# Who sums the two halves of the expert output: GpSimd, or VectorE and TensorE

## The chip, the cores and the metric

The kernel runs on one core of a Trainium2 chip, as one launch. The metric is the device time of that launch in microseconds (us), the median of several executions.

## What is computed

Two layers, each a graph attention over 2708 nodes with 256 features followed by a mixture of experts of which every row uses two. The change lies behind the last experts, in the last lines of layer 1:

```python
    def _L1_ffn_ref(x, gate_w, gate_b, w1, b1, w2, b2, gamma, beta):
        ...
        topk_vals, topk_idx = jax.lax.top_k(gate_logits, K)
        topk_w = jax.nn.softmax(topk_vals, axis=-1)
        h = jax.nn.relu(jnp.einsum('bsh,ehf->bsef', x, w1) + b1)
        expert_out = jnp.einsum('bsef,efh->bseh', h, w2) + b2
        sel = jnp.take_along_axis(expert_out, topk_idx[:, :, :, None], axis=2)
        moe = jnp.sum(topk_w[..., None] * sel, axis=2)
        y = x + moe
        mu = jnp.mean(y, axis=-1, keepdims=True)
        var = jnp.var(y, axis=-1, keepdims=True)
        return (y - mu) / jnp.sqrt(var + EPS) * gamma + beta
    ...
    x = x + _L1_ffn_ref((_layernorm(x, axis=-1))[None], ...)[0]
```

## The kernel before

The 2708 rows lie in 22 tiles: 20 of 128 rows, and tiles 20 and 21 of 74 rows each. The rows of layer 1 are sorted by expert into pages of 128, called blocks; 45 blocks (0 to 44) are computed in the main stream, and further ones only if the data needs them.

**A block.** TensorE makes the hidden activations (`hide`, L880) and the output (`sum_hidden`, L895 and L898). VectorE multiplies the output by the row's weight on its way out of PSUM (`scaled`, L902 and L904). GpSimd issues an indirect DMA that adds the 128 result rows to an array in DRAM (`add`, L909). There are two such arrays, `sums1[0]` for even blocks and `sums1[1]` for odd ones; an add into one of them waits until the previous add into the same one has landed (`last_add`). `sums1[0]` also holds the input rows, stored there before. So y of a row is `sums1[0] + sums1[1]`, and the layer norm over y is what is left to do.

**The three groups of tiles.** `EARLY_LAST` names two groups that finish while blocks still run: tiles 0 to 5 behind block 35, and tiles 6 to 11 behind block 38. `early_last` waits for the add, and for tiles 6 to 11 also until the last weights and the last rows of the blocks were asked for (`loaded`, `fetched`). It loads both halves of y into `y_all`, a view of the old mask's memory (the profile calls it `mask_t`), with L1420: `y_all[:, 0]` and `y_all[:, 1]`. GpSimd adds the halves, two tiles at a time (L1953). VectorE then takes mean and variance (`stats`: L427 and L428), 13 small operations for the inverse deviation, and two operations for each tile (L1963, L1965). The other ten tiles, 12 to 21, are `late_last`: four groups of 2, 2, 4 and 2 tiles. `load_y` asks for them behind the last block and behind the conditional. `last1` then lets GpSimd add the halves by pairs (L1990), VectorE take the statistics, ScalarE the first inverse root (`root`, L434 and L435), VectorE one Newton step (`mend`, three operations at L380), and VectorE two operations for each tile:

```python
                nc.vector.scalar_tensor_tensor(y, y_all[:r, 0, t], ln_y.mv[:r, t, 0:1],
                                               last["gamma"][:r], op0=OP.subtract, op1=OP.mult)
                nc.vector.scalar_tensor_tensor(y, y, ln_y.rstd[:r, t:t + 1], x1[:r, t, :],
                                               op0=OP.mult, op1=OP.add)
```

These are L2003 and L2005. Each pair then leaves by a store from SP's queue (L2008). The stores of tiles 6 to 11 (`early_out`, L1974) are issued on SP behind the loads of `load_y`.

**The conditional.** `experts1.rest` (L940 to L943) holds the blocks past 44 under a `tc.If`. Each engine loads the number of rows in use, compares and, as a rule, jumps over the body. An engine that jumps raises its semaphores by what the body would have raised them; that is what a row of L943 in the trace shows. GpSimd raises those of its DMA queue there too (`INC_SWDGE_SEM`). Whoever waits behind the conditional for work that could have been in the body waits for that row.

**What sets the order.** Instructions of one engine run in the order in which they are issued. That order is made by a planner in the kernel's own text, `Clock`: pieces of work are generators which yield an engine and a cost (`yield "POOL", 1.3`), a `Mark` that something is done, or a slot of a buffer (`Slots`), and the planner issues what would be ready first. `clock.moved` says when a transfer should land. The planned times shape the order only; what an instruction really waits for are semaphores. `psum_stage` opens a new set of PSUM tiles and closes the old one, so that a new tile's first use waits for the old tiles' last uses.

## Time and profile before

| what | value |
|---|---|
| time, median of 3 runs | 1156.15 us (1155.14 to 1159.67) |
| the profiled execution's own time | 1157.12 us |
| its span | 1155.4 us |
| mean granted TensorE clock | 0.949 |
| TensorE matmul busy | 1030.2 us, 89% of the span |
| VectorE busy | 542.2 us, 47% |
| ScalarE busy | 573.1 us, 50% |
| GpSimd busy | 366.2 us, 32% |

The span is that of the instructions on the core; the execution's own time holds 1.7 us more around it. TensorE's share is that of the whole kernel. The last 43 us are a stage of another kind: TensorE's last matmul of the profiled execution starts at 1112.1 us. All times of the prediction are counted from the start of the span.

### The profile page before, as it was taken

To read this page: it belongs to the slowest core of one execution; us is meant where nothing else is said; L and a number is where in the kernel's file an instruction comes from. 1 tells how busy PE (TensorE), PEld (TensorE's weight loads), DVE (VectorE), ACT (ScalarE), POOL (GpSimd) and SP (SyncE) were. 2 spreads that over 40 slices of the span, in tenths; PEclk is the share of its full clock that TensorE was granted. 3 is DMA by queue.
4 is the path that set the end of the run, shared out by engine and by line. 5 is a ranking of instruction groups with operands and counts; after the bars stand their busy time and mean duration, and the time that the engine had idled before them with its cause. 6 is when DMAs were issued, how large, how long until landed. Compare 5 with 4: busy or idle time off the path is not lost. (4 is left out here: it accounts for less than half of the span.)

```text
span 1155.4 us, 21226 instructions
## 1 busy us (share of the span) xinstructions
PE 1030.2 (89%) x6665; PEld 914.1 (79%) x6665; DVE 542.2 (47%) x2083; ACT 573.1 (50%) x1599; POOL 366.2 (32%) x417
## 2 busy tenths in 40 slices
PE   5999999997999999999999998998984888899850
PEld 3888888875789999999998954998984777798840
DVE  7678888865531111101111336647776641122368
ACT  4876667653534444444443458446753543344420
POOL 7521121111142221112223351252434355333441
PEclk9999999998999999999999999998996899899985
DMA  9965445410898999999899959401125477787973
GB/s 281 288 236 174 156 159 182 135 77 28 295 283 263 322 322 327 324 304 321 250 318 332 335 155 256 153 1 38 60 65 186 122 180 187 171 214 176 282 196 120
DMA packets 165053, 238.96 MB, mean 207 GB/s; under 512 B 10627, under 2 KB 139966, under 8 KB 162224
## 3 DMA queue, kind: packets, MB, share of 16 engines
q1 hardware_dynamic: 146116, 214.09, 56.6%
q0 software_dynamic: 18816, 23.42, 10.6%
q8 instruction: 56, 0.92, 0.3%
q14 instruction: 65, 0.53, 0.1%
HBM read 205.54 MB, written 54.99 MB: 225 GB/s over the span
## 5 line engine op out<-in xcount | busy, mean ns | idle before, releaser
L904 DVE TENSOR_SCALAR yo<-out_ps,w 128x256 f32<-128x256 f32 x92 | 44.5, 484 | 409.4 <-PE out_ps L898 408.8
L1238 PE MATMUL att_ps<-g_all,z 128*128 128x257 f32 (+3 forms) x968 | 227.3, 388 | 0.0
L1238 PEld LDWEIGHTS att_ps<-g_all,z 128*128 128x128 f32 (+3 forms) x968 | 177.3, 188 | 36.3 <-issue 8.9
L898 PE MATMUL out_ps<-room,ht 128*128 128x256 f32 x872 | 200.0, 381 | 0.0
L880 PEld LDWEIGHTS hid_ps<-xt,room 128*128 128x128 f32 x1504 | 176.2, 193 | 6.3 <-issue 3.4
L880 PE MATMUL hid_ps<-xt,room 128*128 128x128 f32 x1504 | 177.5, 277 | 3.2 <-DMA room<-in_L_ffn_W_dram 2.7
L898 PEld LDWEIGHTS out_ps<-room,ht 128*128 128x128 f32 x872 | 161.9, 191 | 21.0
L1224 ACT ACTIVATE zr<-e_bc,minus_one,g_all 128x256 f32<-128x256 f32 (+3 forms) x242 | 130.5, 591 | 59.0 <-DVE z L1227 58.3
L884 ACT ACTIVATE ht<-hid_ps,w_t 128x128 f32<-128x128 f32 x376 | 128.8, 364 | 26.7 <-PE hid_ps L880 7.4
L909 POOL DMA_INDIRECT sums<-yo,xg x43 | 66.8, 1555 | 233.7 <-DVE side L872 204.7
L674 POOL DMA_INDIRECT rows_d<-xr,place x88 | 92.3, 1049 | 123.7 <-DVE xr L443 77.0
L1638 PE MATMUL att_ps<-half,wide_mask 128*128 128x258 f32 (+1 forms) x968 | 124.5, 290 | 2.5 <-ACT h_all L1575 1.5
L1638 PEld LDWEIGHTS att_ps<-half,wide_mask 128*128 128x128 f32 (+1 forms) x968 | 121.5, 195 | 3.9 <-ACT h_all L1575 2.4
L909 POOL DMA_INDIRECT sums<-yo,xr x45 | 70.7, 1572 | 128.9 <-DVE w L902 42.7
L1227 DVE SCALAR_TENSOR_TENSOR z<-zr,mask_t 128x256 f32<-128x256 f32 (+3 forms) x242 | 96.2, 419 | 30.6 <-ACT zr L1224 17.5
L884 ACT ACTIVATE ht<-hid_ps,w1x 128x128 f32<-128x128 f32 x180 | 62.3, 363 | 95.7 <-PE hid_ps L880 92.5
L874 ACT ACTIVATE w<-xg,side 128x1 f32<-128x1 f32 x43 | 12.7, 294 | 167.5 <-DVE side L872 167.5
L1515 POOL CAST wide_mask<-mask_t 128x1408 fp32r<-128x1408 fp8e4 x31 | 42.5, 1376 | 101.6 <-PE att_ps L1638 67.5
L880 PE MATMUL hid_ps<-lo,wide_mask 128*128 128x128 f32 x480 | 65.7, 294 | 9.9 <-DMA wide_mask<-in_L_ffn_w_dram 9.0
L880 PEld LDWEIGHTS hid_ps<-lo,wide_mask 128*128 128x128 f32 x480 | 62.6, 206 | 13.7 <-issue 10.9
L898 PE MATMUL out_ps<-wide_mask,ht 128*128 128x256 f32 x240 | 60.8, 399 | 0.0
L461 PE MATMUL tr_ps<-ident,xr 128*128 128x128 f32 (+1 forms) x214 | 38.7, 291 | 24.0 <-DMA xr<-rows_d 15.6
(292 smaller groups left out, 1328.3 us busy)
## 6 DMA issues: line engine op xcount, KB each, us to landing
room<-in_L_ffn_W_dram SPq DMA_DIRECT2D x94, 1024.0 KB
wide_mask<-in_L_ffn_w_dram SPq DMA_DIRECT2D x60, 512.0 KB
room<-in_adj_dram SPq DMA_DIRECT2D x20, 1354.0 KB
room<-in_L_ffn_w_dram SPq DMA_DIRECT2D x30, 512.0 KB
rows_d<-nobody SPq DMA_DIRECT2D x1, 7511.0 KB
rows_d<-nobody SPq DMA_DIRECT2D x5, 1295.0 KB
sums<-nobody SPq DMA_DIRECT2D x2, 2944.0 KB
xr<-rows_d SPq DMA_DIRECT2D x45, 129.5 KB
```

The lines of the kernel that those rows point to most:

```text
L461: nc.tensor.transpose(ps[:, c, :r], src[:, c * P:(c + 1) * P], ident[:r, :r])
L674: ins = nc.gpsimd.indirect_dma_start(out=self.rows_d[:, :], in_=self.rows[t][:r], in_offset=None, out_offset=bass.IndirectOffsetOnAxis(ap= ...
L880: nc.tensor.matmul(ps[:, :P], w1_b[:, c, f * P:(f + 1) * P], xt[:, c, :], start=(c == 0), stop=(c == DC - 1))
L884: nc.scalar.activation(ht[:, f, :], ps[:, :P], self.func, bias=self.bias[:, f, b:b + 1])
L898: nc.tensor.matmul(ps[:, :D], ht[:, f, :], self.rooms[b % 3][1][:, f, :], start=False, stop=(f == self.FC - 1))
L904: nc.vector.tensor_scalar(yo, ps[:, :D], w, None, op0=OP.mult)
L909: ins = nc.gpsimd.indirect_dma_start(out=self.sums[k][:, :], in_=yo, in_offset=None, out_offset=bass.IndirectOffsetOnAxis(ap=self.rows.pop ...
L1224: nc.scalar.activation(zr[:k, :n], e_bc[:k, lo:lo + n], AF.Relu, bias=minus_one[:k], scale=g_all[:k, j, D + 1:D + 2])
L1227: nc.vector.scalar_tensor_tensor(z[:k, :n], zr[:k, :n], 1.0, mask_t[:k, j // 2, lo:lo + n, j % 2], op0=OP.add, op1=OP.mult)
L1238: nc.tensor.matmul(accs[i][:r, :D + 1], z[:k, q * P:q * P + r], g_all[:k, j, :D + 1], start=(j == 0), stop=(j == LAST))
L1515: nc.gpsimd.tensor_copy(m, src)
L1638: nc.tensor.matmul(accs[i][:, :D + 2], wide_masks[i, j % 2][:k, j // 2, :], half_k[:k, j, :], start=(j == 0 and half_k is halves[0]), stop ...
```

## The change

The sums of tiles 6 to 11 go from GpSimd to VectorE; those of tiles 0 to 5 stay on GpSimd. For the late ten tiles there is no add: TensorE multiplies both halves by the identity matrix and accumulates them in a PSUM tile, and the two consumers on VectorE (the statistics, and the first of the two operations) read PSUM. A new PSUM stage is opened behind the conditional.

```diff
@@ early_last
         for t in range(lo, lo + n, 2):
-            yield "POOL", 1.3
-            nc.gpsimd.tensor_tensor(y_all[:, 0, t:t + 2], y_all[:, 0, t:t + 2],
-                                    y_all[:, 1, t:t + 2], OP.add)
+            yield ("DVE", 0.75) if lo else ("POOL", 1.3)
+            (nc.vector if lo else nc.gpsimd).tensor_tensor(
+                y_all[:, 0, t:t + 2], y_all[:, 0, t:t + 2], y_all[:, 1, t:t + 2], OP.add)
@@ last1
+        banks = []
         yield y_at
         for pair in two:
-            t, r = pair[0]
-            yield "POOL", 1.3
-            nc.gpsimd.tensor_tensor(y_all[:r, 0, t:t + 2], y_all[:r, 0, t:t + 2],
-                                    y_all[:r, 1, t:t + 2], OP.add)
+            slot = yield from bank.get()
+            ps = ps_tile("y_ps").rearrange("p (q d) -> p q d", d=D)
+            banks.append((ps, slot))
+            yield "PE", 1.2 * len(pair)
+            for q, (t, r) in enumerate(pair):
+                for k in range(2):
+                    nc.tensor.matmul(ps[:r, q], ident[:r, :r], y_all[:r, k, t],
+                                     start=k == 0, stop=k == 1)
             yield "DVE", 1.3
-            for t, r in pair:
-                ln_y.stats(y_all[:r, 0, t], t, r)
+            for q, (t, r) in enumerate(pair):
+                ln_y.stats(ps[:r, q], t, r)
         ...
-        for pair in two:
+        for pair, (ps, slot) in zip(two, banks):
             yield "DVE", 1.9
-            for t, r in pair:
+            for q, (t, r) in enumerate(pair):
                 y = y_all[:r, 1, t]
-                nc.vector.scalar_tensor_tensor(y, y_all[:r, 0, t], ln_y.mv[:r, t, 0:1],
+                nc.vector.scalar_tensor_tensor(y, ps[:r, q], ln_y.mv[:r, t, 0:1],
                                                last["gamma"][:r], op0=OP.subtract, op1=OP.mult)
                 ...
+            clock.set(slot)
@@ behind the conditional
+    psum_stage(wide=5, acc=3)
     clock = Clock()
+    bank = Slots(clock, 5)
```

In the issued order, VectorE's three adds stand behind the weighting of block 43: two of them ahead of that of block 44, the third behind it. TensorE's sums come in the order of tiles 12 and 13, 14 and 15, 16 and 17, 20 and 21, 18 and 19. On VectorE the three Newton operations of tiles 12 and 13 and their four last operations now come directly behind their statistics; before, the statistics of tiles 14 and 15 stood in between. The order on SP is the same as before.

## Prediction

> **What bounds the kernel now.** I read the chain of waits first, for the tail, because the change touches nothing before it.

> ```profile
> 1135.08 0.43 issue
> 1135.51 0.44 DVE bn L427
> ...
> 1151.38 0.48 DVE mask_t L2005
> ```

> (start, us, what.) From 1135.51 to the last operation's end at 1151.86 the chain is VectorE alone; the last store and the end take 3.5 us more, to 1155.4. So what counts is when VectorE gets to the late ten tiles. The timeline tells what kept it:

> ```profile
> 1112.54 0.48 DVE L904 TENSOR_SCALAR yo<-out_ps,w 128x256 f32<-128x256 f32 x1 [1.30 <-PE out_ps L898]
> 1119.07 0.43 DVE L427 BATCH_NORM_STATS2 bn<-mask_t 128x6 f32<-128x256 f32 x1 [6.05 <-POOL mask_t L1953]
> ...
> 1125.40 1.26 POOL L1990 TENSOR_TENSOR mask_t<-mask_t 128x512 f32<-128x512 f32 x1 [3.93 <-DMA mask_t<-sums]
> 1125.52 1.42 DVE L1965 SCALAR_TENSOR_TENSOR mask_t<-mask_t,rstd_y,h_all 128x256 f32<-128x256 f32 x1
> ...
> 1127.38 0.48 DVE L1965 SCALAR_TENSOR_TENSOR mask_t<-mask_t,rstd_y,h_all 128x256 f32<-128x256 f32 x1
> ...
> 1135.51 0.43 DVE L427 BATCH_NORM_STATS2 bn<-mask_t 128x6 f32<-128x256 f32 x1 [0.95 <-DVEq L943]
> ...
> 1136.28 1.26 POOL L1990 TENSOR_TENSOR mask_t<-mask_t 74x512 f32<-74x512 f32 x1 [2.53 <-DMA mask_t<-sums]
> ```

> Two losses. VectorE idles 6.05 us for GpSimd's sums of tiles 6 to 11. Then, each time GpSimd runs an add of the late tiles (1125.40, 1128.26, 1131.09, 1132.3), the VectorE operation beside it takes 1.42 to 1.50 us in place of 0.48: four times, 4.0 us in all. At 1135.51 it has left the conditional (0.95 us) and finds the late tiles summed. GpSimd and SP:

> ```profile
> 1103.10 0.96 SPq L1420 DMA_DIRECT2D mask_t<-sums  x2
> ```

> ```profile
> 1116.20 1.54 POOL L909 DMA_INDIRECT sums<-yo,xr  x1 [0.95 <-SPq L943]
> 1117.20 4.27 POOL L1953 TENSOR_TENSOR mask_t<-mask_t 128x512 f32<-128x512 f32 x3
> ```

> The loads of tiles 6 to 11 were issued at 1103.1 (the trace's completion events: landed 1108.13 and 1111.59), but their sums stand in GpSimd's queue behind the add of block 44, which waits until 1116.20 for an earlier add.

> **Part 1: tiles 6 to 11 on VectorE.** Removed: three GpSimd adds, and 6.05 us of waiting. Added on VectorE: three TENSOR_TENSOR of 512 columns. None of that size is in the trace; TENSOR_TENSOR rows of 96 and 192 columns take 258 and 357 ns, 1.03 ns a column, so 512 take 0.69 us, some 0.62 us start to start. Bounds: 0.55 us (columns alone) and GpSimd's own 1.83 us. I take 0.62, the rows of the same engine.
> Block 43's weighting ends at 1111.18 and the second load has landed at 1111.59, so the first two run from 1111.65 to 1112.9. Block 44's weighting is queued behind them and ends at 1113.45, not 1113.02; its add cannot go before 1116.20, so that is hidden, with 2.4 us of cover. The third add ends at 1114.1. The statistics begin there, not at 1119.07: 5.0 us earlier. From there the same instructions as before, without the four stretches: 9.0 us in all, so the last L1965 ends at about 1125.4, not 1134.56.

> **Part 2: the late sums on TensorE.** Removed: five GpSimd adds, the stretches counted above, and a stall of 0.37 us at 1141.85. Added: 20 matmuls, each of two passes of 256 columns: 40 rows. What starts them? The new PSUM tiles wait for the old ones' last readers, which include VectorE in the conditional's body; so TensorE waits until VectorE has passed L943. The same join in layer 0 shows it:

> ```profile
> PE tr_ps L461 <- DVEq L943: 1.1, 1, 1.1
> ```

> VectorE's L943 row came 0.5 us behind its last operation (1134.56 to 1135.05). So TensorE starts at 1125.9, though the first loads landed at 1125.3 or earlier. And it starts slow:

> ```profile
> 1110.00:1112.00 2.00, 2.00 (x12) 1.67 (x11) 0.54 (x2) 1.08 (x1) 0.74 (x1) 1.00 1.12 319
> ...
> 1126.00:1128.00 2.00, 0.00 (x0) 0.00 (x0) 1.97 (x4) 0.00 (x0) 0.66 (x1) 0.50 1.01 341
> ```

> (Window, length, then busy time and count of PE, PEld, DVE, ACT, POOL; granted clock, DMA share, GB/s.) The clock is 1.00 with the blocks and 0.50 from 1116.2 to the end, as TensorE idles.

> ```profile
> 1108.77 1.89 PE L898 MATMUL out_ps<-wide_mask,ht 128*128 128x256 f32 x8
> ```

> Eight such passes take 1.89 us at full clock (0.216 us apart); at half, as in the stretch from 1002 to 1007 us, twice that, 0.43 us apart. A pair of tiles is eight passes: 3.4 us and 0.2 us to drain. VectorE can read the first pair at 1129.6. Over the whole kernel the clock came back in each case only behind a stretch of some 3.4 us of dense work, so the first pair runs at half throughout and the next two mostly at full (1.7 us each, done by 1131.4 and 1133.1).
> This 3.4 + 0.2 us is the new wait. Before, VectorE went on 0.95 us behind its last L1965; now 4.2 us (1125.4 to 1129.6). Queued behind it is all of VectorE's late work, and the stores.
> VectorE's late work took 16.35 us (1135.51 to 1151.86). Less the stall of 0.37; plus 0.62, since the first Newton step now waits for ScalarE (from the statistics' end at 1136.68 to ScalarE's second row's end at 1137.25) with nothing between; plus 20 operations that read PSUM. The scalar-tensor-tensor row that reads PSUM (`h_all<-att_ps,inv,lo`, L1769) takes 484 ns, L2003 from SBUF 478: 6 ns each. The widest bound is the tensor-scalar row: 484 from PSUM (L904), 410 from SBUF (L443), 74 ns each, 1.5 us. I take 0.2 us, nearest to the same operation. Sum 16.8 us: the end of VectorE goes from 1151.86 to 1146.4, 5.4 us earlier.

> [...]

> **Does the last pair come in time?** VectorE wants tiles 20 and 21 at 1138.0, and 18 and 19, whose sums stand behind them on TensorE, at 1139.1. Loads of tiles 20 and 21 landed at 1136.15 (completion events; two DMA engines alone carry these 74-row loads, 47 ns a packet of 1 KB, all the way since 1123). They start with SP:

> ```profile
> 1121.66 2.99 SPq L1420 DMA_DIRECT2D mask_t<-sums  x6
> ```

> Block 44's add had landed at 1120.04; SP went on when GpSimd's L943 row ended at 1121.66, 0.2 us behind its last L1953. Without L1953 in front, that row may end at 1120.1 to 1120.6 or, if its 1.6 us are its own (1.49 us in layer 0, where an indirect DMA ran in front), at 1121.6. I take 1.2 us earlier: the loads end at 1134.95, their sums at 1136.7. TensorE has then idled since 1133.1; with the clock still full, 18 and 19 are there at 1138.6 and nothing is lost; at half, at 1140.3, 1.2 us are lost. The middle: 0.6 us. SP's other work is no dearer: the stores L1974 of tiles 6 to 11 go out behind the same loads, when VectorE has long finished, and the two slow engines serve them in order.

> **Sum.** 5.4 - 0.6 = 4.8 us less. The profiled execution took 1157.12 us (span 1155.4), 1.0 above the median; I take the difference from the median: 1156.15 - 4.8 = 1151.35.

> **Rivals.**
> (a) The last pair is late. If GpSimd's 1.6 us at L943 stay, TensorE gets tiles 20 and 21 at 1136.15, its clock has dropped, the sums are done at 1139.3 and 1141.5; VectorE stalls 1.2 us twice: gain 3.1, 1153.1 us. For it: 1.49 us in layer 0. Against: SP's start 0.2 us behind L1953's end.
> (b) TensorE stays at half clock through all 40 passes: 17.1 us from 1125.95, so tiles 18 and 19 are ready at 1143.25, and 7.5 us of VectorE work stand behind them: 1150.7, gain 1.1, 1155.0 us. Against: dense work brought the clock back in every earlier stage.
> (c) TensorE need not wait for VectorE's L943. Then it starts as the first pair lands (1124.1), VectorE goes on at 1127.8: gain 7.2, 1149.0 us. Against: the layer 0 row.
> (d) Slower. Block 44's weighting is queued behind two adds that wait for the load of tiles 6 to 11. Past 2.4 us of lateness (landing after 1114.0) its add on GpSimd, the late loads and all else move with it; past 7.2 us (landing after 1118.8) the gain is gone. That load took 8.07 us from its issue at 1103.52; at twice that it lands at 1119.7 and the kernel is 0.9 us slower, 1157.0. For it: a 6.4 us landing of block 40's add beside these loads. Against: before and after are alike until then.
> (e) The halves are not summed where the text says: the issued order shows they are; no chance to speak of.

> **How the numbers follow.** Forecast 0.56 (own range 1150 to 1152.8), (a) 0.22, (b) 0.08, (c) 0.08, (d) 0.06. A measurement of this kernel tells about 0.5% (5.8 us) from no change. Beyond it lie (c) and, as executions differ by some 0.3%, about a third of the forecast: faster 0.28. Slower by over 0.5% would need (d) with 13 us of lateness or a disturbance: 0.04. Same 0.68. The range takes in (c) and (b): 1148.8 to 1155.1.

> **What would show it.** Right: no row of VectorE over 0.7 us behind 1112; statistics of tiles 6 to 11 from about 1114; a TensorE wait on VectorE's L943, then eight passes at clock 0.50 and 0.43 us apart; VectorE idle some 4.2 us there. SP's L1420 before 1121 is right for the early start, at 1121.6 for (a). Wrong: matmuls before VectorE's L943 (c), clock 0.50 on the last pairs (b), block 44's add after 1116.5 (d).

## The result, and the profile after

| what | before | after |
|---|---|---|
| time, median of 20 runs each | 1155.27 us (1150.15 to 1161.28) | 1154.63 us (1149.98 to 1157.1) |
| ratio after to before | | 0.9978, 95% interval 0.9963 to 0.9994 |
| the profiled execution's own time, its span | 1157.12, 1155.4 us | 1155.89, 1154.2 us |

The kernel became 0.22% faster, 2.5 us of 1156 (interval 0.7 to 4.3 us), where 4.8 us were forecast. The ratio with its interval is the record's estimate from all 40 runs; the two medians alone lie 0.64 us apart and the means 1.9, so the gain is known no better than its interval. Executions differ by several us ahead of the point that the change touches: block 44's add landed at 1120.06 us before and at 1121.39 after. So the two traces are laid on that landing. **The tail**, from it to the span's end, took 35.34 us before and 32.79 after, 2.55 us less. That this is just the gain of the ratio is partly luck: a second trace of the changed kernel, below, has a tail of 34.02 us, 1.3 us less than before.

The timeline of the changed kernel, VectorE, TensorE and SP mixed (start, us, engine, line, operation; in brackets the idle time before it and what ended it):

```profile
1112.69 1.29 DVE L1953 TENSOR_TENSOR mask_t<-mask_t 128x512 f32<-128x512 f32 x2
...
1115.14 0.42 DVE L427 BATCH_NORM_STATS2 bn<-mask_t 128x6 f32<-128x256 f32 x1
...
1122.99 2.99 SPq L1420 DMA_DIRECT2D mask_t<-sums  x6
...
1125.97 0.49 DVE L1965 SCALAR_TENSOR_TENSOR mask_t<-mask_t,rstd_y,h_all 128x256 f32<-128x256 f32 x1
...
1127.21 8.41 PE L1995 MATMUL y_ps<-mask_t,ident 128*128 128x256 f32 x26 [13.30 <-DVEq L943]
...
1131.06 0.43 DVE L427 BATCH_NORM_STATS2 bn<-y_ps 128x6 f32<-128x256 f32 x1 [4.60 <-PE y_ps L1995]
...
1138.11 4.93 PE L1995 MATMUL y_ps<-mask_t,ident 74*74 74x256 f32 x14 [2.48 <-DMA mask_t<-sums]
...
1140.29 0.43 DVE L427 BATCH_NORM_STATS2 bn<-y_ps 74x6 f32<-74x256 f32 x1 [0.65 <-PE y_ps L1995]
...
1143.08 0.43 DVE L427 BATCH_NORM_STATS2 bn<-y_ps 128x6 f32<-128x256 f32 x1 [1.61 <-PE y_ps L1995]
```

VectorE adds the halves (L1953), and takes the statistics of tiles 6 to 11 without the 6.05 us of idle time; its last L1965 ends at 1126.46, 5.1 us behind block 44's landing; before it was 14.5 us behind. Then three waits for TensorE stand in the place of GpSimd's sums: 4.60, 0.65 and 1.61 us. SP's first late load is issued at 1122.99, 1.6 us behind the landing, as before (1121.66 behind 1120.06). The chain of waits of the changed kernel (start, us, what) says what lies behind the two small ones:

```profile
1126.47 11.59 DMA mask_t<-sums
1138.06 0.04 issue
1138.11 4.95 PE y_ps L1995 x14
1143.05 0.02 issue
1143.08 0.44 DVE bn L427
```

The end hangs on the loads of tiles 20 and 21, then on TensorE's last 14 passes, and on VectorE only from 1143.08. The busy time by windows of the changed kernel (window, its length, then busy time and count of PE, PEld, DVE, ACT, POOL; granted clock, DMA share, GB/s):

```profile
1128.00:1130.00 2.00, 2.00 (x6) 1.55 (x6) 0.00 (x0) 0.00 (x0) 0.00 (x0) 0.50 1.01 342
1132.00:1134.00 2.00, 2.00 (x11) 1.73 (x10) 1.26 (x7) 0.50 (x2) 0.00 (x0) 0.99 0.52 196
1136.00:1138.00 2.00, 0.00 (x0) 0.00 (x0) 1.83 (x10) 0.50 (x2) 0.00 (x0) 1.00 0.44 164
1138.00:1140.00 2.00, 1.89 (x6) 1.29 (x7) 1.58 (x4) 0.00 (x0) 0.00 (x0) 0.71 0.12 45
1140.00:1142.00 2.00, 2.00 (x6) 1.59 (x5) 1.10 (x4) 0.47 (x2) 0.00 (x0) 0.50 0.37 138
```

The first pair runs at clock 0.50 (six passes touch the 2 us from 1128, 11 those from 1132). The clock is back at 1132, TensorE has nothing to do from 1136 to 1138, and the clock falls again in 1138 to 1140, just as the last two pairs run.

### The profile page after: what moved, and what is told of

It is laid out like the page before. It is cut to its first block, busy times and chain, and to the rows that moved or that the text cites. A ratio compares the mean times of both kernels' runs of the same rounds, so it can differ in the third digit from the quotient of the medians.

```text
span 1154.2 us, 21299 instructions
## 1 busy us (share of the span) xinstructions
PE 1042.8 (90%) x6705; PEld 923.3 (80%) x6705; DVE 541.7 (47%) x2086; ACT 572.2 (50%) x1599; POOL 357.2 (31%) x409
## 3 DMA queue, kind: packets, MB, share of 16 engines
q0 software_dynamic: 18816, 23.42, 10.6%
## 5 line engine op out<-in xcount | busy, mean ns | idle before, releaser
L904 DVE TENSOR_SCALAR yo<-out_ps,w 128x256 f32<-128x256 f32 x92 | 44.5, 484 | 408.5 <-PE out_ps L898 407.8
L898 PE MATMUL out_ps<-room,ht 128*128 128x256 f32 x872 | 201.0, 383 | 0.0
L898 PEld LDWEIGHTS out_ps<-room,ht 128*128 128x128 f32 x872 | 162.7, 192 | 21.3
L909 POOL DMA_INDIRECT sums<-yo,xg x43 | 66.8, 1554 | 234.1 <-DVE side L872 195.3
L909 POOL DMA_INDIRECT sums<-yo,xr x45 | 71.1, 1579 | 127.3 <-DMA sums<-yo,xr 35.2
L1227 DVE SCALAR_TENSOR_TENSOR z<-zr,mask_t 128x256 f32<-128x256 f32 (+3 forms) x242 | 96.5, 420 | 29.7 <-ACT zr L1224 18.0
L461 PE MATMUL tr_ps<-ident,xr 128*128 128x128 f32 (+1 forms) x214 | 38.9, 292 | 24.7 <-DMA xr<-rows_d 16.3
L898 PE MATMUL out_ps<-wide_mask,ht 128*128 128x256 f32 x240 | 60.6, 398 | 0.0
```

The lines of the kernel that those rows point to most:

```text
L461: nc.tensor.transpose(ps[:, c, :r], src[:, c * P:(c + 1) * P], ident[:r, :r])
L898: nc.tensor.matmul(ps[:, :D], ht[:, f, :], self.rooms[b % 3][1][:, f, :], start=False, stop=(f == self.FC - 1))
L904: nc.vector.tensor_scalar(yo, ps[:, :D], w, None, op0=OP.mult)
L909: ins = nc.gpsimd.indirect_dma_start(out=self.sums[k][:, :], in_=yo, in_offset=None, out_offset=bass.IndirectOffsetOnAxis(ap=self.rows.pop ...
L1227: nc.vector.scalar_tensor_tensor(z[:k, :n], zr[:k, :n], 1.0, mask_t[:k, j // 2, lo:lo + n, j % 2], op0=OP.add, op1=OP.mult)
```

## The experiments

In each kernel the same sums are computed; only who does them, how they are loaded (in two kernels also stored), and what stands beside them differ. Each line is one traced execution. Times are us from block 44's landing, taken as the start of GpSimd's row at L943 that waits for it; the add's last completion event comes 0.02 to 0.03 us earlier. "First read" is VectorE's first statistics of the late tiles, "stalls" its waits for sums or loads behind that (not the 0.60 us for ScalarE that every kernel with part 2 has).

| kernel | last load of tiles 20, 21 | first read | stalls | VectorE's end | tail |
|---|---|---|---|---|---|
| before | 16.1 | 15.4 | 0 | 31.8 | 35.3 |
| after | 16.7 | 9.7 | 2.3 | 29.3 | 32.8 |
| after, once more | 17.0 | 9.3 | 3.9 | 30.5 | 34.0 |
| part 1 alone | 16.3 | 6.4 | 1.4 | 26.3 | 29.9 |
| part 1 alone, timed | 16.4 | 8.3 | 0 | 27.7 | 31.3 |
| part 2 alone | 16.3 | 14.9 | 0 | 32.0 | 35.6 |
| after, 56 busy matmuls before the conditional | 16.3 | 10.3 | 2.2 | 29.9 | 33.5 |
| after, loads cut | 13.3 | 10.2 | 0 | 27.3 | 30.8 |
| after, old PSUM stage | 16.4 | 8.1 | 1.9 | 27.3 | 30.9 |
| all on VectorE, cut | 12.8 | 6.0 | 0.2 | 25.7 | 29.2 |
| all on VectorE, cut, timed | 13.6 | 6.6 | 0.2 | 26.3 | 29.7 |
| after, loads cut, 56 busy matmuls behind the conditional | 14.5 | 12.0 | 0 | 29.2 | 32.7 |
| after, loads cut, 30 busy matmuls there | 12.4 | 8.5 | 0 | 25.6 | 29.1 |
| first pair on VectorE, loads cut | 13.5 | 6.5 | 2.4 | 26.2 | 29.7 |

**Part 1 alone** (VectorE sums tiles 6 to 11; the late sums stay on GpSimd, without the new PSUM stage). The difference from the changed kernel, shortened:

```diff
...
             yield ("DVE", 0.75) if lo else ("POOL", 1.3)
             (nc.vector if lo else nc.gpsimd).tensor_tensor(
...
-                    nc.tensor.matmul(ps[:r, q], ident[:r, :r], y_all[:r, k, t],
-                                     start=k == 0, stop=k == 1)
+            nc.gpsimd.tensor_tensor(y_all[:r, 0, t:t + 2], y_all[:r, 0, t:t + 2],
+                                    y_all[:r, 1, t:t + 2], OP.add)
```

> Part 1 alone: VectorE sums tiles 6 to 11, GpSimd still sums the late ten. Measure: the stretch from the landing of block 44's add to the end of the span (35.4 us before, 32.8 after). My theory (the first part carries the gain; the second costs a 4 us wait for TensorE and leaves its last pairs late): VectorE is at tiles 12 and 13 at 6.5 us behind that landing, two of its operations are stretched by 1 us each, it ends some 26.6 us behind the landing, and the stretch is 30.1 us, shorter than with both parts. Rival (the second part carries the gain by taking GpSimd away from VectorE): the stretch is 33 us or more.

Measured: tail 29.94 us, 5.4 less than before and 2.9 less than with both parts. The timeline of this kernel shows what GpSimd's sums still cost:

```profile
1119.58 1.26 POOL L1990 TENSOR_TENSOR mask_t<-mask_t 128x512 f32<-128x512 f32 x1 [7.26 <-DMA mask_t<-sums]
...
1120.87 0.43 DVE L427 BATCH_NORM_STATS2 bn<-mask_t 128x6 f32<-128x256 f32 x1 [1.77 <-POOL mask_t L1990]
```

Once VectorE is no longer late, the first pair's sum by GpSimd takes 1.26 us and VectorE waits 1.77; TensorE's sum of the same pair makes it wait 4.60. Part 1 carries the gain: the next experiment has part 2 without it, and a second execution of part 1 stands at the end.

**Part 2 alone** (GpSimd sums tiles 6 to 11 as before, TensorE the late tiles):

```diff
-            yield ("DVE", 0.75) if lo else ("POOL", 1.3)
-            (nc.vector if lo else nc.gpsimd).tensor_tensor(
-                y_all[:, 0, t:t + 2], y_all[:, 0, t:t + 2], y_all[:, 1, t:t + 2], OP.add)
+            yield "POOL", 1.3
+            nc.gpsimd.tensor_tensor(y_all[:, 0, t:t + 2], y_all[:, 0, t:t + 2],
+                                    y_all[:, 1, t:t + 2], OP.add)
```

> Part 2 alone: GpSimd sums tiles 6 to 11, TensorE the late ten. Same measure (35.4 us before, 32.8 after). My theory: VectorE ends tiles 6 to 11 about 10.5 us behind the landing, TensorE begins 0.5 us later and takes 3.8 us for the first pair, so VectorE goes on at 14.8 us and nothing is late behind it: 35.1 us, hardly less than before. Rival (the second part carries the gain): 33 us or less.

Measured: tail 35.64 us; nothing is gained against 35.34. The timeline of this kernel:

```profile
1120.93 0.43 DVE L427 BATCH_NORM_STATS2 bn<-mask_t 128x6 f32<-128x256 f32 x1 [6.03 <-POOL mask_t L1953]
...
1123.40 2.99 SPq L1420 DMA_DIRECT2D mask_t<-sums  x6
...
1136.72 0.43 DVE L427 BATCH_NORM_STATS2 bn<-y_ps 128x6 f32<-128x256 f32 x1 [4.26 <-PE y_ps L1995]
```

Both waits stand in one row after the other: 6.03 us for GpSimd, 4.26 for TensorE. What the missing GpSimd adds save (the stretched VectorE rows, 4.0 us), the second wait takes. And SP's loads start at 1123.40, 1.6 us behind the landing at 1121.80, with GpSimd's adds in front; without them (part 1 alone, after) the distance is the same 1.6. GpSimd's semaphore row at L943 started with the landing and took 1.60 us in all 14 traces, whether GpSimd stood idle there or was still adding.

**Busy work on TensorE** (a product of the identity that nobody reads, ahead of the conditional, to hold the clock):

```diff
+    busy = ps_tile("busy_ps")
+    for _ in range(56):
+        nc.tensor.matmul(busy[:, :P], ident, ident, start=True, stop=True)
     experts1.rest()
```

> The changed kernel, with 56 matmuls of the identity by itself (into a PSUM tile that nobody reads) between the last block and the conditional, so that TensorE's clock is still full when the sums begin. If TensorE's slow start sets the end, the stretch from the landing of block 44's add to the end falls from 32.8 us by the 1.9 us that the first pair gets faster: 30.9 us. My theory: the end is set by the loads of tiles 20 and 21, which land 16.7 us behind that add; the faster first pairs only leave TensorE idle for longer before them, the clock drops, and both last pairs are summed at half: 32.5 to 34.5 us, no gain.

Measured: 33.51 us, within the band, but it does not test the clock cleanly. TensorE's timeline in this kernel:

```profile
1106.31 12.67 PE L2028 MATMUL busy_ps<-ident 128*128 128x128 f32 x112
1122.14 5.85 PE L1995 MATMUL y_ps<-mask_t,ident 128*128 128x256 f32 x26 [3.16 <-PEq L943]
1130.25 5.94 PE L1995 MATMUL y_ps<-mask_t,ident 74*74 74x256 f32 x14 [2.26 <-DMA mask_t<-sums]
```

TensorE's wait for its own L943 (3.16 us) stood behind the busy work, so the sums began at 8.2 us in place of 5.8. At full clock (the 26 passes took 5.85 us, 0.22 us each) the first pair took 2.06 us from its first pass to VectorE's read; in the changed kernel it took 3.85. In the last pairs the clock had fallen again (14 passes in 5.94 us, 0.42 us each), and they stalled VectorE by 2.24 us.

**74-row loads cut** into rows 0 to 63 and 64 to 73 (shortened; the loads of 128 rows stay as they are):

```diff
...
+            for a, b in ((0, 64), (64, TAIL)):
+                nc.sync.dma_start(y_all[a:b, k, lo:lo + 2], src[a:b])
```

> The changed kernel, with each load of the 74 rows of tiles 20 and 21 cut in two, rows 0 to 63 and 64 to 73. My theory (these loads run on two DMA engines and land last, and TensorE's last sums and 2.3 us of VectorE's waiting hang on them): with all 16 engines the last load lands about 12 us behind block 44's add, not 16.7, VectorE does not wait for the last pairs, and the stretch falls from 32.8 us to 30.5 us. Rival (the loads land late because of the bytes ahead of them, or TensorE's clock alone makes the last sums late): the last landing stays at 16 us or the stretch at 32 us or more.

Measured: tail 30.79 us, 2.0 less than after. Of the waits of VectorE, one for TensorE is left (waited for: us in total, times, longest):

```profile
DVE bn L427 <- PE y_ps L2000: 4.6, 1, 4.6
DVE yo L904 <- PE out_ps L898: 2.0, 1, 2.0
DVE mask_t L1953 <- DMA mask_t<-sums: 0.9, 1, 0.9
DVE stat L380 <- ACT rstd_y L435: 0.6, 1, 0.6
```

The last load lands at 13.3 us in place of 16.7, and both late stalls (0.65 and 1.61) are gone. A 128-row load has 16 completion events. In the changed kernel a 74-row load has one early event (at 5.2 us for one load, 7.5 for the other) and then only two, at 12.8 and 13.5 us, at 15.9 and 16.7. Cut, the 64-row pieces have 16 events and the 10-row pieces ten behind an early one. In the trace of before the DMA share, a mean over 16 engines, is 1.01 from 1126 to 1128, with the 128-row loads under way, and 0.14 from 1133 to 1135, when only the 74-row loads move: 2.2 engines. Why 74 rows go to two engines, and why 64 and 10 rows have 16 and ten events, is not shown. The cut has a price that is easily missed: the last 128-row load, of tiles 16 to 19, landed at 10.6 to 11.5 us in the eight traces with whole loads, and at 11.6 to 13.7 in the six with cut ones.

**The old PSUM stage** (TensorE then waits for no reader in the conditional on VectorE):

```diff
-    psum_stage(wide=5, acc=3)
     clock = Clock()
     bank = Slots(clock, 5)
```

> The changed kernel without the new PSUM stage: the sums use the old stage's tiles, so TensorE no longer waits for VectorE behind the conditional. Tail = from the landing of block 44's add to the span's end (changed kernel 32.8 us). My theory: TensorE starts with the first landing, 5.1 us behind block 44's instead of 5.8, VectorE waits 3.9 us in place of 4.6, and nothing of it arrives at the end, since the last pairs wait for the loads that land 16.7 us behind: tail 32.8, within 0.3. Rival, case (c) of the prediction: the join with VectorE was worth 2.4 us: tail 30.4.

Measured: tail 30.94 us, nearer to the rival's 30.4 than to my 32.8. The timeline of this kernel:

```profile
1145.67 6.52 PE L1995 MATMUL y_ps<-mask_t,ident 128*128 128x256 f32 x18 [12.20 <-DMA mask_t<-sums]
...
1149.46 0.43 DVE L427 BATCH_NORM_STATS2 bn<-y_ps 128x6 f32<-128x256 f32 x1 [3.50 <-PE y_ps L1995]
...
1157.85 3.25 PE L1995 MATMUL y_ps<-mask_t,ident 74*74 74x256 f32 x14 [2.48 <-DMA mask_t<-sums]
...
1159.41 0.43 DVE L427 BATCH_NORM_STATS2 bn<-y_ps 74x6 f32<-74x256 f32 x1 [1.36 <-PE y_ps L1995]
...
1161.14 0.43 DVE L427 BATCH_NORM_STATS2 bn<-y_ps 128x6 f32<-128x256 f32 x1 [0.56 <-PE y_ps L1995]
```

TensorE now waits for the load, not for VectorE, and VectorE for 3.50 us in place of 4.60. Yet VectorE again stalls at both last pairs, so its end is set by TensorE's last 14 passes, which start at 16.5 us (after: 16.7). They took 3.25 us here and 4.93 there: the clock stayed at 1.00 (the same columns as in the windows above, for this kernel):

```profile
1157.00:1159.00 2.00, 1.15 (x6) 0.80 (x7) 1.01 (x3) 0.00 (x0) 0.00 (x0) 1.00 0.17 63
1159.00:1161.00 2.00, 2.00 (x10) 1.51 (x8) 1.10 (x4) 0.35 (x2) 0.00 (x0) 1.00 0.37 137
```

These 1.7 us and the 0.2 of the earlier start are the whole 1.9 us; the first pair, read 1.6 us earlier, gave nothing that arrived at the end. So the theory had the join's effect on the first pair about right (the start came at 4.3 us, 0.8 earlier than expected) and left out the clock. Whether the clock stayed up because TensorE started earlier, or by its phase, is not separated here; the next run bears on it.

**After, once more**, unaltered:

> The changed kernel once more, unaltered, to see what in its tail belongs to the kernel and what to the execution. My theory: SP's first late load is 1.6 us behind block 44's landing and the loads of tiles 20 and 21 land 16 to 17 us behind it, as in every run so far; the granted clock changes in steps of 3.4 us whose phase differs from execution to execution, so the first pair's wait (4.6 us before) may be 3.6 to 4.8 and the two stalls of the last pairs together (2.26 before) 1.2 to 2.5: tail 31.2 to 33.2. Rival: the clock's steps follow TensorE's own work alone: wait 4.6 and stalls 2.2 to 2.3 again, tail 32.7 to 32.9.

Measured: tail 34.02 us, above my band; wait 4.21, stalls 2.07 and 1.81. The timeline of this execution:

```profile
1162.45 5.82 PE L1995 MATMUL y_ps<-mask_t,ident 74*74 74x256 f32 x14 [2.48 <-DMA mask_t<-sums]
...
1165.32 0.43 DVE L427 BATCH_NORM_STATS2 bn<-y_ps 74x6 f32<-74x256 f32 x1 [2.07 <-PE y_ps L1995]
...
1168.31 0.43 DVE L427 BATCH_NORM_STATS2 bn<-y_ps 128x6 f32<-128x256 f32 x1 [1.81 <-PE y_ps L1995]
...
1165.00:1167.00 2.00, 2.00 (x6) 1.54 (x5) 1.10 (x4) 0.44 (x2) 0.00 (x0) 0.50 0.01 3
```

The last line is one of this execution's windows. The same 14 passes behind the same load took 5.82 us: the clock was at 0.50 from 15.5 to 22.3 us, and they ran from 17.0 to 22.9. So 3.25, 4.93 and 5.82 us are one piece of work under three phases of the clock (its steps fall at different points of that work); the direction of the theory holds, its band was too narrow. The rival, the same stalls again, falls.

**All sums on VectorE**, loads and stores of the 74-row tiles cut, without the new PSUM stage (the difference from the changed kernel, shortened):

```diff
...
-                    nc.tensor.matmul(ps[:r, q], ident[:r, :r], y_all[:r, k, t],
-                                     start=k == 0, stop=k == 1)
+            nc.vector.tensor_tensor(y_all[:r, 0, t:t + 2], y_all[:r, 0, t:t + 2],
+                                    y_all[:r, 1, t:t + 2], OP.add)
```

> All sums of tiles 6 to 21 on VectorE, nothing on GpSimd or TensorE; loads and stores of the 74-row tiles cut into rows 0 to 63 and 64 to 73. My theory: VectorE waits only some 0.5 us for the first landing, none for sums or loads, and pays 5 adds of 0.65 us for the late tiles: its end is 4.1 + 2.3 - 3.2 = 3.2 us before that of the changed kernel (29.3 us behind the landing), 26.1, tail 29.6, about as good as part 1 alone with GpSimd's adds (29.9). Rival: VectorE's own adds cost as much as GpSimd's (1.26 us each): tail 32.7.

Measured: tail 29.16 us. The waits of VectorE in this kernel:

```profile
DVE yo L904 <- PE out_ps L898: 1.3, 1, 1.3
DVE mask_t L1995 <- DMA mask_t<-sums: 0.9, 2, 0.7
```

0.9 us of waiting for loads is all that is left in the tail; VectorE works through. Its five adds of some 0.65 us, 3.2 us in all, cost less than the 4.60 us that it waits for TensorE's first pair alone when the loads are cut (tail 30.8). The cut stores have little part in it: from VectorE's end to the span's end it is 3.4 us here and 3.5 there.

**Busy work behind the conditional**, loads cut as above, first with 56 and then with 30 matmuls:

```diff
     experts1_scope.close()
+    busy = ps_tile("busy_ps")
+    for _ in range(56):
+        nc.tensor.matmul(busy[:, :P], ident, ident, start=True, stop=True)
     psum_stage(wide=5, acc=3)
```

> The changed kernel with the 74-row loads cut into rows 0 to 63 and 64 to 73 (tail 30.8 as it stands) and 56 matmuls of the identity between the conditional and the new PSUM stage, whose result nobody reads and which end some 5 us behind block 44's landing. My theory: the clock is at 1.00 when the first pair's passes start, at 5.8 as before; they take 1.7 us in place of 3.4; VectorE waits 2.6 to 2.9 us in place of 4.6; tail 28.7 to 29.1. Rival: the first pair's wait is the join with VectorE and the loads, not the clock: wait 4.3 or more, tail 30.5 to 31.

Measured: tail 32.67 us, a miss. TensorE's L943 took 3.43 us behind block 44, the busy work ran in part at half clock (0.50 in the window 1138:1140 of this trace, just behind its start at 1137.96), and ended at 9.9 us; VectorE waited 7.15. What holds in it: at full clock (1.00 in the windows from 1150 to 1154) the first pair was read 2.06 us behind its first pass.

> As the run before with busy matmuls and cut 74-row loads, with 30 of them in place of 56, so that they end before the join with VectorE (which frees TensorE 5.8 us behind block 44's landing). My theory: the first pair's passes start at 5.8 at clock 1.00 and VectorE reads them at 7.9 in place of 9.7 to 10.2; from that read to VectorE's end it was 17.1 us both with and without busy work, so the end is at 25.0 and the tail 28.6, within 0.6. Rival: the loads of tiles 14 to 19 are no earlier than before and hold the next pairs: tail 30 or more although the first pair is early.

Measured: tail 29.11 us, first read 8.5 us. The timeline of this kernel:

```profile
1133.85 9.77 PE L2036 MATMUL busy_ps<-ident 128*128 128x128 f32 x60 [3.21 <-PEq L943]
...
1143.78 0.67 PE L2000 MATMUL y_ps<-mask_t,ident 128*128 128x256 f32 x2 [0.16 <-PE busy_ps L2036]
...
1144.84 3.72 PE L2000 MATMUL y_ps<-mask_t,ident 128*128 128x256 f32 x16 [0.39 <-DMA mask_t<-sums]
...
1146.49 0.43 DVE L427 BATCH_NORM_STATS2 bn<-y_ps 128x6 f32<-128x256 f32 x1 [3.47 <-PE y_ps L2000]
```

The first passes start at 5.8 us at full clock (1.00 in the windows from 1140 to 1146 of this trace); the second half of the load, which landed at 6.8 us here, then holds them for 0.39 us. The read is 1.7 us earlier than with cut loads alone (10.2), and the tail 1.7 us shorter: 1.1 us is VectorE's shorter wait (3.47 for 4.60), 0.6 us is that VectorE came to it earlier in this execution. The rival, that the loads hold the next pairs, falls: VectorE has no stall behind the first read.

**The first late pair on VectorE, the other four on TensorE**, loads cut (shortened):

```diff
...
+        if lo == 12:
+            nc.vector.tensor_tensor(y_all[:, 0, lo:lo + 2], y_all[:, 0, lo:lo + 2],
+                                    y_all[:, 1, lo:lo + 2], OP.add)
+        for pair in two if lo > 12 else ():
```

> The changed kernel with the 74-row loads cut, and the first late pair (tiles 12 and 13) summed on VectorE; the other four pairs stay on TensorE. My theory: VectorE has work when TensorE has not: it adds at the first landing (5.1 us behind block 44's), is through with tiles 12 and 13 at 9.8, and waits until 11.2 for tiles 14 and 15, which TensorE sums at half clock from 7.6 to 11.0; with the changed kernel and cut loads that point lies at 14.4: tail 30.8 - 3.2 = 27.6, within 0.6. Rival: the loads or the stores, not VectorE, set the end by now: tail 30 or more.

Measured: tail 29.74 us, 2.1 more than expected. The timeline of this kernel:

```profile
1145.51 0.43 DVE L427 BATCH_NORM_STATS2 bn<-y_ps 128x6 f32<-128x256 f32 x1 [0.46 <-PE y_ps L2008]
...
1147.06 5.02 PE L2008 MATMUL y_ps<-mask_t,ident 128*128 128x256 f32 x22 [0.73 <-DMA mask_t<-sums]
...
1148.66 0.43 DVE L427 BATCH_NORM_STATS2 bn<-y_ps 128x6 f32<-128x256 f32 x1 [1.96 <-PE y_ps L2008]
```

The second pair came as expected (11.1 us); the third waits 1.96 us, as its load landed only at 12.6 us, against 11.0 in the changed kernel, whose loads are whole. The rival has a part in it: with VectorE early, the loads are the next to be late.

**Timed.** Part 1 alone and all on VectorE, 12 runs each against 23 of before on the same chip (median 1175.91 us there):

> Part 1 alone, timed. Its tail was 5.4 us shorter than that of the kernel before (29.9 against 35.3), that of the changed kernel 2.5 (measured 2.5 us by the median ratio). My theory: 0.9953 of the time before, interval within 0.9935 to 0.9975, so better than the changed kernel. Rival: the tail of one execution was luck, and part 1 alone is no better than both parts: 0.998.

> All sums of tiles 6 to 21 on VectorE, 74-row loads and stores cut, timed. Its tail was 6.2 us shorter than that of the kernel before. My theory: 0.9947 of the time before, interval within 0.993 to 0.9965, the best of the versions. Rival: no better than the changed kernel's 0.998.

Measured: part 1 alone 0.9953 (0.9932 to 0.9974), all on VectorE 0.9958 (0.9935 to 0.9982). Both are faster than before. Part 1 alone came out as expected; the other gained less than its tail had promised, and is no better than part 1 alone. Their intervals overlap that of the changed kernel (0.9963 to 0.9994), which was taken against other runs: that they beat it rests on the tails, two executions of each, 29.2 to 31.3 us against 32.8 and 34.0, and is not settled by the times alone. Part 1's second tail is 1.4 us longer than its first. There VectorE's first add had to wait for the load of tiles 6 to 11, and its last L1965 ended at 7.7 us in place of 4.6 (waits of VectorE: us in total, times, longest):

```profile
DVE mask_t L1953 <- DMA mask_t<-sums: 1.8, 1, 1.8
```

GpSimd's first late add then ran beside one of these rows, which took 1.37 us.

## Why the prediction was right and where it failed

The forecast was 4.8 us; the traces give 2.55 and the times 2.5. The sign, "within 0.5%" and the range hold; the forecast gain lies outside the measured interval. The range was wide enough for rivals (b) and (c), so a time inside it does not speak for the mechanism. The steps do: one failed, a term built on it failed with it, and one was mis-sized. Step by step, in the prediction's own terms, from block 44's landing:

- **Part 1: right.** Adds of 0.68 us for a row of 512, two in 1.29 (512 columns at 1.03 ns are 0.53 us, not the 0.55 of the lower bound). The last L1965 was to end 5.4 us behind the landing; it ended at 5.1. No single VectorE operation behind 1112 took over 0.7 us.
- **TensorE waits for VectorE's L943, then eight passes at half clock: right.** The read was to come at 9.6 us, and came at 9.7 (wait 4.2 forecast, 4.60 measured). That the new stage makes TensorE wait is shown by the old stage, where that wait is gone. The clock came back 4.8 us behind the first pass, not 3.4; VectorE did not wait for TensorE there, so it cost nothing.
- **Reading PSUM: right.** L2008 takes 0.48 us, as from SBUF, 0.51 us start to start in both kernels; the statistics are 0.446 us apart from the next operation in place of 0.433. In all 0.1 us, with 0.2 forecast.
- **VectorE's late work: 17.3 us, not 16.8.** From the first read to the end it took 19.6, of which 2.26 are stalls. In the four kernels with part 2 that had no late stalls it took 17.1, so 0.3 us are the work itself and 0.2 came with the stalls. The term for ScalarE was sound (0.60 us measured; the two times named are 0.57 apart, not 0.62). The subtracted "stall of 0.37 us at 1141.85" was none. It was a piece called "issue" in the chain of waits of before; the timeline of before has the next operation 0.40 us behind that L2005, as behind the other L2005 rows:

```profile
1140.89 0.48 DVE L2005 SCALAR_TENSOR_TENSOR mask_t<-mask_t,rstd_y,h_all 128x256 f32<-128x256 f32 x1
1141.30 0.48 DVE L2003 SCALAR_TENSOR_TENSOR mask_t<-mask_t,mv_y,gamma 128x256 f32<-128x256 f32 x1
1141.81 0.48 DVE L2005 SCALAR_TENSOR_TENSOR mask_t<-mask_t,rstd_y,h_all 128x256 f32<-128x256 f32 x1
1142.21 0.42 DVE L427 BATCH_NORM_STATS2 bn<-mask_t 128x6 f32<-128x256 f32 x1
```

- **"I take 1.2 us earlier: the loads end at 1134.95": this step failed.** GpSimd's 1.6 us at L943 are its own, as rival (a) had it; SP started 1.6 us behind the landing in all runs. The argument against (a), SP's start 0.2 us behind the end of L1953, was a coincidence, and the trace of before shows it: the semaphore row had begun at the landing, beside the third add (first line: its lengths in ns, its first and last start; second line: GpSimd's last two adds).

```profile
L943 POOLq INC_SWDGE_SEM  x2: 1490/1543/1596, 671.7 to 1120.1; - x2
1118.42 3.04 POOL L1953 TENSOR_TENSOR mask_t<-mask_t 128x512 f32<-128x512 f32 x2
```

Tiles 20 and 21 landed at 16.7 us, not at 14.9: 1.2 us of that is SP's start, 0.6 is that the loads took longer than in the trace of before (16.1; 16.3 to 17.0 in the other kernels with whole loads).

- **"The middle: 0.6 us", built on it: this term measured 2.26** (0.65 and 1.61; rival (a) had 2.4). With the loads cut, landing at 13.3 us, the stalls are nought: the late load is what they hang on. A load at 14.9 us was not tried, so whether 0.6 us would have been right for it stays open. The term was also taken as one number where it is several: the last pairs' passes depend on the clock's phase, and stalls of 1.9, 2.3 and 3.9 us came of it.

For this one execution the difference adds up: 1.66 us from the last pairs (2.26 - 0.6), 0.53 from VectorE's work, 0.1 from the first read, 2.3 in all, where 2.25 are missing. In the second execution the stalls alone were 1.6 us longer.

Rival (a) thus took place, with a gain 0.5 us below its 3.1 for the work mis-sized above. Rival (b) did not: the clock came back 10.6 us behind the landing. Its sign, clock 0.50 on the last pairs, was there all the same, as the clock had fallen again; it does not tell (b) from (a). (c) did not: TensorE waited for L943. (d) did not, though its sign, block 44's add after 1116.5, came too (1117.65): block 43's weighting, ahead of the change, already ended 1.4 us later (1112.59 for 1111.18), and block 44's add started 3.0 us behind the end of its weighting, so the weighting did not hold it up.

What the prediction never asked was what each part would give by itself. Part 2 was costed as the removal of GpSimd's adds from a kernel in which VectorE was late; part 1 had already taken most of that loss away. Against part 1 alone, part 2 takes away waits for GpSimd of 3.2 us and two rows stretched by 0.9 and 1.0 us (in part 1's second execution no waits, but four rows stretched, by 3.9 us in all), and brings waits of 6.9 us for TensorE (8.1 in the second execution) and 0.6 for ScalarE. The tails with both parts were 1.5 to 4.1 us longer than those with part 1 alone.

## What to carry to other kernels

Cost each part of a change on top of the other and not only against the kernel as it stands: a wait that one part removes can't be earned again by the second. Moving short work to an idle engine pays only if that engine is ready: count its clock, what it must wait for to get its buffers, and how long its first result takes, against doing the work at once on the engine that needs it. And where a stall ends in a load, look at how many engines carry that load before anything is rearranged around it.
